# Layer 3 of a four-layer graph network: ScalarE's second measuring pass beside the propagation, and another order of copies and passes between the two steps

## Chip, cores and metric

The kernel runs on one core of one Trainium2 chip. The metric is device time in microseconds of one execution; the time before is the median of three executions. The profile is of one further execution.

## The reference, cut to what matters

Four layers follow one another, each as x = x + layer(relu(layernorm(x))), on N = 3327 nodes with D = 256 features. The change is in the fourth, called layer 3:

```python
def _top_p_attention(X, W1, W2, W3):
    logits = (X @ W1.T @ W2.T) @ (X @ W3.T).T
    probs = softmax(logits, axis=-1)
    # keep the largest probabilities of a row until their sum reaches 0.9
    A = probs * mask
    return A / max(A.sum(-1, keepdims=True), 1e-12)

R = (S + eye) / (S + eye).sum(-1, keepdims=True)     # S is adj
Z, Xf, Xa = 0, X, X
for n in range(2):
    A = _top_p_attention(Xa, W1, W2, W3)
    Xf = R @ Xf                       # propagation
    Xa = A @ Xa                       # attention
    Z = Z + Xf @ U1[n].T + Xa @ U2[n].T
out = layernorm(X + Z) * ln_g + ln_b
```

All arithmetic of these products is in float32.

## The kernel before

The nodes are padded to 3328 and cut into T = 26 blocks of 128 rows. A "row" below is such a block, m = 0 to 25. Layer 3 has two steps, 0 and 1, and every row of a step needs four pieces of work.

1. **Logits and exponentials.** `prepare` / `logits_steps`: TensorE multiplies queries and centred keys (L913) in four chunks, each into a two-bank PSUM tile `pl`; ScalarE takes the exponential of each chunk into the row tile `e` of 128 x 3328 with a running sum (L934). The tile pool `ps_row` behind `pl` has two buffers, which `pkq` (keys and queries of the next step), `u` (products with U1 and U2) and `pl` share.
2. **The search for the row's threshold.** `search_steps` is a generator with three stops. Up to the first stop, VectorE sums the row (`total`, L951) and ScalarE turns it into a first threshold `t` by four small activations with one VectorE operation between them (L952 to L956). Then comes ScalarE's first measuring pass, a Relu over the whole row (L967, `short`), and a second stop; then its second pass, a Sign over the whole row (L972, `sign`), and a third stop. In row 0 of a step, `alone` holds, and VectorE does the second one (L970). The rest is VectorE's: L977 to L980 improve the threshold, L983 measures again over the row, L992 and L996 mask the row in four parts and take the largest eight of each block, L1001 and L1004 take the largest forty, and L1012 applies the final threshold to `e`, the "mask" of the row.
3. **Attention.** `rows_times_steps` transposes `e` in 7 groups of up to four blocks on TensorE (L177) into PSUM, ScalarE copies each group to SBUF as `eT` (L180; three buffers, two PSUM buffers), and TensorE multiplies them with the values (L188). `Rows.begin` issues the first two groups' transposes, `Rows.finish` the rest.
4. **Propagation.** `propagated_steps` multiplies 26 blocks of the transposed adjacency with the features (L1068). SyncE's queue loads them in two slabs.

In step 0 the propagated row is scaled by ScalarE (`xf`, L1109), transposed and copied (`PropagationOfFirstStep.turn`, L138), and multiplied with U1 (`sums`, L1121; copied by ScalarE to `fsa`, L1123). The attention row is scaled (L1079), transposed and copied to `xT_a` (`AttentionOfFirstStep.turn`, L138), turned into keys and queries of step 1 (`node`; copies at L249 and L253 and a small DMA on ScalarE's queue), and multiplied with U2 (`values`).

**What sets the order.** Under `manual_schedule` TensorE's order is the order in which the code is traced. The orders of the other engines come from a planner that gives each instruction its place by estimated times and priorities; `high_priority` raises a priority. `issue_after(ins)` lets the instructions of its block stand only behind `ins` on its engine. `run(steps, at)` walks a generator and calls what `at` lists at a step number, so that other work is interleaved.

In step 0, rows 0 to 18 are "interleaved": `rows.finish(m)` runs together with the search of row m + 2, and then `propagate_first(m + 4)` together with the logits of row m + 3, at steps 0 and 12, the attention row's `turn` at step 3, `node` at 9, `values` at 18 and `rows.begin(m + 1)` at 20. Rows 19 to 25 have no propagation beside them except the last two. The function `passes` puts the search beside `rows.finish`: both passes each behind the newest `eT` copy, at steps 0 and 2, and VectorE's part at step 3.

Between the steps, the propagation of row 24 runs with the first logits of step 1, then a branch (`if_failed`) repairs rows whose search failed, and then the search of row 0 of step 1 and the propagation of row 25 follow, with the logits of rows 1 and 2 of step 1 at its steps 0, 6, 14 and 20. In step 1 each row does `rows.finish(m)` with a search, and then `propagate_second(m)` with the logits of row m + 3.

Of the kernel before, what the change touches and what calls it, by code (L numbers as in the profile page):

```python
# [16 lines left out]
AF = mybir.ActivationFunctionType  # L17
# [8 lines left out]
T = 26  # L26
NP = T * P
LAST = N - (T - 1) * P
NC = D // P
# [16 lines left out]
def kernel(  # L46
# [22 lines left out]
    nc = tc.nc  # L69
# [49 lines left out]
    def run(steps, at=None):  # L119

        for k in steps:
            for what in (at or {}).get(k, ()):
                what()

    def merged(*plans):
        out = {}
        for p in plans:
            for k, v in p.items():
                out.setdefault(k, []).extend(v)
        return out  # L130

    def transposed(src, pool, name):

        pt = ps_tr.tile([P, 4, P], F32, tag="tr", name=f"pt_{name}")
        for c in range(NC):
            nc.tensor.transpose(pt[:, c, :], src[:, c * P : (c + 1) * P], ident)
        dst = pool.tile([P, NC, P], F32, tag="xT", name=f"xT_{name}")
        nc.scalar.copy(dst, pt[:, :NC, :])  # L138
        return dst

    def search(es, t_bits, top_bit, measure, target, pool, name):
# [20 lines left out]
        nc.vector.scalar_tensor_tensor(eq, rank, n_tied, eq, ALU.is_lt, ALU.mult)  # L162
        nc.vector.scalar_tensor_tensor(e, eq, t, e, ALU.mult, ALU.add)

    last_turned = []
    GROUPS = [range(g, min(g + 4, T)) for g in range(0, T, 4)]

    def rows_times_steps(new_acc, e, rhs, pool, name):
# [671 lines left out]
    def layer_3_in(tag, big, ep, w3, sm3, h3, kT0, ksum0, left, at_end):  # L840
# [90 lines left out]

        def exp_of_logits(step, m, kT, e, parts, name=""):
            def evict(c, dst, src):
                nc.scalar.activation(dst, src, AF.Exp, accum_out=parts[:, c : c + 1])  # L934

            return logits_steps(kT, qT[:, m * P : (m + 1) * P], e, f"{name}{tag}{step}_{m}", evict)

# [332 lines left out]
        AHEAD = 3  # L1270
        EARLY = 4
        LATE = 3


        with tc.manual_schedule(engines=PE_ALONE):

            st0, made, dens, props = new_state("0"), {}, {}, []

            def prepare(step, m, kT):
                made[m] = scores(step, m, kT)  # L1280
                return made[m][2]

            def find(step, m, st):
                return search_steps(step, m, *made[m][:2], st, dens, m == 0)

            def passes(finder):


                if finder is None:
                    return {}  # L1290
                next(finder)

                def one_more():
                    with tc.issue_after(last_turned[-1].ins):
                        next(finder, None)

                return {0: [one_more], 2: [one_more], 3: [lambda: next(finder, None)]}

            def propagate_first(m, at):
                acc = new_acc(f"f0_{m}")  # L1300
                run(propagated_steps(acc, 0, m, h3), at)
                props.append(PropagationOfFirstStep(m, acc))

            def spread(steps, first=0, second=10):

                return {k: [lambda: next(steps, None)] for k in (first, second)}

            class Rows:


                def __init__(self, step, values):
                    self.step, self.values, self.begun = step, values, {}

                def begin(self, m):
                    if m < T:
                        name = f"a{self.step}_{m}"
                        accs = []

                        def acc():
                            accs.append(new_acc(name))  # L1320
                            return accs[0]

                        steps = rows_times_steps(acc, made.pop(m)[0], self.values, w3, name)
                        next(steps)
                        self.begun[m] = steps, accs

                def finish(self, m, at=None):
                    steps, accs = self.begun.pop(m)
                    run(steps, at)
                    return accs[0]  # L1330

            for i in range(EARLY):
                plan = {}
                if props:
                    p = props.pop(0)
                    plan = {5: [p.turn], 16: [p.sums]}
                if i == 0:
                    left.pool = w3, "eT", 3
                    propagate_first(0, dict(zip((14, 20), ([what] for what in left.stages))))
                    mean0 = key_sum(kT0, ksum0, "0")  # L1340
                elif i == 1:
                    steps = prepare(0, 0, kT0)
                    centred = {3: [lambda: centre(kT0, mean0(), "0")]}
                    propagate_first(1, merged(centred, spread(steps, 9, 19), plan))
                    run(find(0, 0, st0))
                else:
                    propagate_first(i, merged(spread(prepare(0, i - 1, kT0)), plan))
                    finder = find(0, i - 1, st0)
                    if i + 1 < EARLY:
                        run(finder)  # L1350
            p = props.pop(0)
            p.turn()
            p.sums()
            rows = Rows(0, h3)
            rows.begin(0)
            left_over = {}
            for m in range(T):
                plan = merged(passes(finder), left_over)
                if props:
                    p = props.pop(0)  # L1360
                    plan = merged(plan, {1: [p.turn], 5: [p.sums]})
                interleaved = m + EARLY < T - LATE
                steps = iter(())
                if m + AHEAD < T and not interleaved:
                    def begin_logits():
                        nonlocal steps
                        steps = prepare(0, m + AHEAD, kT0)
                        next(steps)

                    plan = merged(plan, {4: [begin_logits], 6: [lambda: next(steps)]})  # L1370
                a = AttentionOfFirstStep(m, rows.finish(m, plan), dens.pop(m), f"{m}")
                if interleaved:
                    left_over = {}
                    steps = prepare(0, m + AHEAD, kT0)
                    after = {3: [a.turn], 9: [a.node], 18: [a.values], 20: [lambda: rows.begin(m + 1)]}
                    propagate_first(m + EARLY, merged(spread(steps, 0, 12), after))
                elif m + 2 < T:
                    rows.begin(m + 1)
                    a.turn()
                    left_over = {0: [a.node], 2: [a.values]}  # L1380
                elif m + 1 < T:
                    left_over = {}
                    after = {1: [a.turn], 4: [a.node], 8: [a.values], 22: [lambda: rows.begin(m + 1)]}
                    propagate_first(T - LATE, after)
                finder = find(0, m + AHEAD, st0) if m + AHEAD < T else None


            flags0, mean1 = [], []

            def centre_second():  # L1390
                mean1.append(centre(kT1, total1(), "1"))

            def sum_second():
                nonlocal total1
                total1 = key_sum(kT1, ksum1, "1")

            def first_flags():
                with tc.high_priority():
                    flags0.extend(failed("0", st0))

            total1 = None
            steps = prepare(1, 0, kT1)
            propagate_first(T - LATE + 1, {
                1: [a.turn], 3: [first_flags], 4: [a.node], 8: [a.values, sum_second],
                11: [centre_second], 17: [lambda: next(steps)], 22: [lambda: next(steps)],
            })
            first_e, first_parts = made[0][:2]
# [17 lines left out]
        with tc.manual_schedule(engines=PE_ALONE):  # L1425
            st1 = new_state("1")
            run(find(1, 0, st1))
            p = props.pop(0)
            plan = {2: [p.turn], 10: [p.sums]}
            propagate_first(  # L1430
                T - 1, merged(spread(prepare(1, 1, kT1), 0, 6), spread(prepare(1, 2, kT1), 14, 20), plan)
            )
            run(find(1, 1, st1))
            finder = find(1, 2, st1)
            p = props.pop(0)
            p.turn()
# [8 lines left out]
            rows.begin(0)  # L1445
            flags1 = []
            for m in range(T):
                acc = rows.finish(m, passes(finder))
                y = attention_of_second_step(m, acc, dens.pop(m), f"{m}")
                plan = spread(prepare(1, m + AHEAD, kT1)) if m + AHEAD < T else {}  # L1450
                plan = merged(plan, {20: [lambda: rows.begin(m + 1)]})
                if m == T - 1:
                    plan = {4: [lambda: flags1.extend(failed("1", st1))]}
                finish3(m, y, propagate_second(m, plan), f"{m}")
                finder = find(1, m + AHEAD, st1) if m + AHEAD < T else None
# [79 lines left out]
```

## Time and profile before

| What | us |
|---|---|
| Median of 3 executions | 2659.49 (2658.65 to 2665.4) |
| The profiled execution, its own time | 2657.14 |
| Its span in the profile | 2655.3 |
| Period of a row in step 0 (rows 1 to 18) | 33.96 |
| Period of a row in step 1 (rows 4 to 22) | 29.31 |
| First transpose of row 0, step 0 | 1026.15 |
| First transpose of row 20, step 0 | 1689.40 |
| First transpose of row 0, step 1 | 1886.43 |

A period is the distance of the first transposes (L177) of two neighbouring rows. Times inside the execution count from the start of the span. In the timeline, a row has the start, the busy time, the engine, the line, the operation, what it writes and reads with shapes, how many instructions are merged, and in brackets the engine's idle time before it and what ended it. PE is TensorE's matmuls, PEld its weight loads, DVE VectorE, ACT ScalarE, POOL GpSimd, SP SyncE; a letter q marks an engine's instruction queue. A float32 matmul stands as two instructions.

### The profile page before, as it was taken

The numbers are of one execution on the slowest core, as the hardware profiler recorded it, in microseconds if no ns is written. First come the engines' busy times: TensorE is split into PE (matmuls) and PEld (weight loads), VectorE is DVE, ScalarE is ACT, GpSimd is POOL, SyncE is SP. The second block draws the span as 40 slices with busy tenths as digits, with TensorE's granted clock in tenths as the row PEclk, the third lists the DMA queues.
The fourth block names the chain that finished last, engine by engine and source line by source line (L and its number), as shares of the span: only waits on it lengthen the run. The fifth ranks groups of instructions, "written<-read, shape, count | busy, mean of one in ns | idle before, by whom it ended". The sixth has DMA issues, their size and how long they took to land. (4 is left out here: it accounts for less than half of the span.)

```text
span 2655.3 us, 42726 instructions
## 1 busy us (share of the span) xinstructions
PE 2575.5 (97%) x15979; PEld 2215.1 (83%) x15979; DVE 2050.0 (77%) x5495; ACT 1030.1 (39%) x1873; POOL 222.6 (8%) x435
## 2 busy tenths in 40 slices
PE   7999999999999999999999999989899999999997
PEld 6999999999999987777777777667677887888786
DVE  6667788888877849766666666893988888888882
ACT  2110134333011134555455555663554455445441
POOL 2000010000000000000000000000021112111111
PEclk9999999999999999999999999999999999999998
DMA  6555555555666631111111111001121122122211
GB/s 224 146 156 168 167 153 176 173 175 157 192 197 199 193 109 68 52 61 61 61 61 61 61 61 61 34 9 67 56 70 64 65 89 70 64 71 83 70 64 52
DMA packets 141359, 273.45 MB, mean 103 GB/s; under 512 B 15427, under 2 KB 67904, under 8 KB 141120
## 3 DMA queue, kind: packets, MB, share of 16 engines
q1 hardware_dynamic: 115648, 252.49, 29.8%
q10 hardware_dynamic: 25472, 17.92, 2.2%
q8 instruction: 132, 2.16, 0.3%
q14 instruction: 107, 0.88, 0.1%
HBM read 248.20 MB, written 20.45 MB: 101 GB/s over the span
## 5 line engine op out<-in xcount | busy, mean ns | idle before, releaser
L188 PE MATMUL a<-h3a,eT_a 128*128 128x256 f32 x1352 | 324.3, 381 | 12.4 <-ACT eT_a L180 11.0
L1068 PE MATMUL f<-h3a,slab3a 128*128 128x256 f32 x1352 | 326.9, 384 | 5.4 <-ACTq L1253 5.3
L188 PE MATMUL a<-vs,eT_a 128*128 128x256 f32 x1352 | 322.7, 383 | 1.1 <-ACT eT_a L180 0.9
L1068 PE MATMUL f<-fsa,slab3a 128*128 128x256 f32 x1352 | 312.7, 382 | 0.0
L1068 PEld LDWEIGHTS f<-h3a,slab3a 128*128 128x128 f32 x1352 | 247.3, 190 | 68.3 <-issue 30.9
L1068 PEld LDWEIGHTS f<-fsa,slab3a 128*128 128x128 f32 x1352 | 249.8, 189 | 52.7 <-issue 17.4
L188 PEld LDWEIGHTS a<-h3a,eT_a 128*128 128x128 f32 x1352 | 245.2, 189 | 53.9 <-ACT eT_a L180 21.5
L996 DVE MAX8 cand_a<-w 128x8 f32<-128x128 f32 x1352 | 281.9, 279 | 6.7
L188 PEld LDWEIGHTS a<-vs,eT_a 128*128 128x128 f32 x1352 | 246.1, 190 | 38.7 <-ACT eT_a L180 7.8
L519 PE MATMUL acc_a<-tsa,s_a 128*128 128x128 f32 (+1 forms) x2028 | 268.4, 275 | 0.7 <-DVE tsa L331 0.7
L180 ACT COPY eT_a<-pt_a 128x512 f32<-128x512 f32 (+1 forms) x364 | 195.0, 552 | 177.1 <-PE pt_a L177 173.6
L934 ACT ACTIVATE e_a<-pl_a 128x1024 f32<-128x1024 f32 x208 | 177.8, 860 | 198.3 <-PE pl_a L913 198.3
L519 PE MATMUL acc_a<-tsa,a_a 128*128 128x128 f32 x2028 | 250.3, 275 | 1.8 <-DVE tsa L334 1.8
L519 PE MATMUL acc_a<-rhs,a_a 128*128 128x128 f32 (+1 forms) x2028 | 250.4, 276 | 0.0
L519 PEld LDWEIGHTS acc_a<-tsa,s_a 128*128 128x128 f32 x2028 | 247.4, 192 | 1.2 <-DVE tsa L331 1.0
L519 PEld LDWEIGHTS acc_a<-tsa,a_a 128*128 128x128 f32 x2028 | 239.1, 192 | 3.1 <-DVE tsa L334 2.2
L519 PEld LDWEIGHTS acc_a<-rhs,a_a 128*128 128x128 f32 x2028 | 238.4, 192 | 1.9 <-ACT rhs L411 0.4
L992 DVE SCALAR_TENSOR_TENSOR w<-e_a,t_a 128x896 f32<-128x896 f32 x208 | 224.9, 1081 | 5.3
L177 PE MATMUL pt_a<-ident,e_a 128*128 128x128 f32 x1352 | 199.5, 273 | 1.8
L177 PEld LDWEIGHTS pt_a<-ident,e_a 128*128 128x128 f32 x1352 | 165.2, 140 | 39.5 <-ACT eT_a L180 9.5
L983 DVE SCALAR_TENSOR_TENSOR w<-e_a,t_a 128x3328 uint8<-128x3328 f32 x52 | 191.9, 3691 | 3.6
L1012 DVE SCALAR_TENSOR_TENSOR e_a<-e_a,all_least 128x3328 f32<-128x3328 f32 x52 | 192.1, 3695 | 1.2
(208 smaller groups left out, 3316.0 us busy)
## 6 DMA issues: line engine op xcount, KB each, us to landing
slab3a<-in_adj_t_dram SPq DMA_DIRECT2D x104, 832.0 KB, 5.9
a_a<-in_adj_t_dram SPq DMA_DIRECT2D x312, 256.0 KB, 3.4
a_a<-in_adj_t_dram SPq DMA_DIRECT2D x156, 320.0 KB, 3.5
x_dram<-x_a ACTq DMA_DIRECT2D x39, 256.0 KB, 2.8
x_a<-x_dram SPq DMA_DIRECT2D x26, 256.0 KB, 3.1
hT_dram<-xT_a ACTq DMA_DIRECT2D x26, 128.0 KB, 3.6
hT<-hT_dram SPq DMA_DIRECT2D x26, 128.0 KB, 2.1
z_dram<-z SPq DMA_DIRECT2D x26, 128.0 KB, 1.7
```

What stands on the lines that cost most here:

```text
L177: nc.tensor.transpose(pt[:, j, :], e[:, k * P : (k + 1) * P], ident)
L180: last_turned.append(nc.scalar.copy(eT[:, : len(blocks), :], pt[:, : len(blocks), :]))
L188: nc.tensor.matmul(acc[:, :width], ready[g][:, j, :], rhs[:, k, :], start=(k == 0), stop=(k == T - 1))
L519: nc.tensor.matmul(self.acc[:, g, at : at + wide], quads[n][:, k - CUTS[c][0], :], t, start=(k == 0 and n in (1, 4)), stop=(k == H - 1 and ...
L934: nc.scalar.activation(dst, src, AF.Exp, accum_out=parts[:, c : c + 1])
L983: nc.vector.scalar_tensor_tensor(junk, e, t, e, ALU.is_lt, ALU.mult, accum_out=got)
L992: nc.vector.scalar_tensor_tensor(w[:, : (b - a) * P], eg, t, eg, ALU.is_lt, ALU.mult, accum_out=below[:, g : g + 1])
L996: nc.vector.max(cand[:, 8 * k : 8 * k + 8], w[:, (k - a) * P : (k - a + 1) * P])
L1012: nc.vector.scalar_tensor_tensor(e, e, least, e, ALU.is_ge, ALU.mult, accum_out=st["kept"][:, m : m + 1])
L1068: nc.tensor.matmul(acc[:, :D], slab[g][:, j, :], xf[:, k, :], start=(n == 0), stop=(n == T - 1))
```

## The change

A function `passes_apart` takes the place of `passes` for the interleaved rows of step 0 and for rows 0 to 22 of step 1. The first pass stays beside `rows.finish`, at its step 0. The second pass, and the VectorE part behind it, go into the propagation that follows: in step 0 at its step 4, behind the newest copy that `transposed` made, in step 1 at its step 1, behind the newest exponential. Two lists hold those copies and exponentials.

Between the steps, `PropagationOfFirstStep(24)` (its scaling copy `xf` and its load of `hT`) is made after the branch and after the search of row 0, instead of before the branch. The search of row 1 is no longer traced after the propagation of row 25 but inside it: its sum and threshold at step 8 with high priority, its first pass there behind the newest exponential, its second pass at step 15 behind the newest exponential; only VectorE's part stays after the propagation. The `sums` of row 24 stay at step 10.

```diff
@@ -129,13 +129,15 @@
                 out.setdefault(k, []).extend(v)
         return out
 
+    last_copied, last_turned, last_exp = [], [], []
+
     def transposed(src, pool, name):
 
         pt = ps_tr.tile([P, 4, P], F32, tag="tr", name=f"pt_{name}")
         for c in range(NC):
             nc.tensor.transpose(pt[:, c, :], src[:, c * P : (c + 1) * P], ident)
         dst = pool.tile([P, NC, P], F32, tag="xT", name=f"xT_{name}")
-        nc.scalar.copy(dst, pt[:, :NC, :])
+        last_copied.append(nc.scalar.copy(dst, pt[:, :NC, :]))
         return dst
 
     def search(es, t_bits, top_bit, measure, target, pool, name):
@@ -162,7 +164,6 @@
         nc.vector.scalar_tensor_tensor(eq, rank, n_tied, eq, ALU.is_lt, ALU.mult)
         nc.vector.scalar_tensor_tensor(e, eq, t, e, ALU.mult, ALU.add)
 
-    last_turned = []
     GROUPS = [range(g, min(g + 4, T)) for g in range(0, T, 4)]
 
     def rows_times_steps(new_acc, e, rhs, pool, name):
@@ -931,7 +932,7 @@
 
         def exp_of_logits(step, m, kT, e, parts, name=""):
             def evict(c, dst, src):
-                nc.scalar.activation(dst, src, AF.Exp, accum_out=parts[:, c : c + 1])
+                last_exp.append(nc.scalar.activation(dst, src, AF.Exp, accum_out=parts[:, c : c + 1]))
 
             return logits_steps(kT, qT[:, m * P : (m + 1) * P], e, f"{name}{tag}{step}_{m}", evict)
 
@@ -1296,9 +1297,25 @@
 
                 return {0: [one_more], 2: [one_more], 3: [lambda: next(finder, None)]}
 
+            def passes_apart(step, finder):
+
+
+                if finder is None:
+                    return {}, {}
+                first = passes(finder)[0]
+
+                def second():
+                    with tc.issue_after((last_copied if step == 0 else last_exp)[-1].ins):
+                        next(finder, None)
+                    next(finder, None)
+
+                return {0: first}, {4 if step == 0 else 1: [second]}
+
             def propagate_first(m, at):
                 acc = new_acc(f"f0_{m}")
                 run(propagated_steps(acc, 0, m, h3), at)
+                if m == T - 2:
+                    return acc
                 props.append(PropagationOfFirstStep(m, acc))
 
             def spread(steps, first=0, second=10):
@@ -1355,11 +1372,12 @@
             rows.begin(0)
             left_over = {}
             for m in range(T):
-                plan = merged(passes(finder), left_over)
+                interleaved = m + EARLY < T - LATE
+                plan, later = passes_apart(0, finder) if interleaved else (passes(finder), {})
+                plan = merged(plan, left_over)
                 if props:
                     p = props.pop(0)
                     plan = merged(plan, {1: [p.turn], 5: [p.sums]})
-                interleaved = m + EARLY < T - LATE
                 steps = iter(())
                 if m + AHEAD < T and not interleaved:
                     def begin_logits():
@@ -1373,7 +1391,7 @@
                     left_over = {}
                     steps = prepare(0, m + AHEAD, kT0)
                     after = {3: [a.turn], 9: [a.node], 18: [a.values], 20: [lambda: rows.begin(m + 1)]}
-                    propagate_first(m + EARLY, merged(spread(steps, 0, 12), after))
+                    propagate_first(m + EARLY, merged(spread(steps, 0, 12), after, later))
                 elif m + 2 < T:
                     rows.begin(m + 1)
                     a.turn()
@@ -1400,7 +1418,7 @@
 
             total1 = None
             steps = prepare(1, 0, kT1)
-            propagate_first(T - LATE + 1, {
+            acc = propagate_first(T - 2, {
                 1: [a.turn], 3: [first_flags], 4: [a.node], 8: [a.values, sum_second],
                 11: [centre_second], 17: [lambda: next(steps)], 22: [lambda: next(steps)],
             })
@@ -1425,12 +1443,26 @@
         with tc.manual_schedule(engines=PE_ALONE):
             st1 = new_state("1")
             run(find(1, 0, st1))
-            p = props.pop(0)
-            plan = {2: [p.turn], 10: [p.sums]}
+            p = PropagationOfFirstStep(T - 2, acc)
+
+            def sum_of_second():
+                nonlocal second
+                second = find(1, 1, st1)
+                with tc.high_priority():
+                    next(second)
+                with tc.issue_after(last_exp[-1].ins):
+                    next(second)
+
+            def signs_of_second():
+                with tc.issue_after(last_exp[-1].ins):
+                    next(second)
+
+            second = None
+            plan = {2: [p.turn], 8: [sum_of_second], 10: [p.sums], 15: [signs_of_second]}
             propagate_first(
                 T - 1, merged(spread(prepare(1, 1, kT1), 0, 6), spread(prepare(1, 2, kT1), 14, 20), plan)
             )
-            run(find(1, 1, st1))
+            run(second)
             finder = find(1, 2, st1)
             p = props.pop(0)
             p.turn()
@@ -1445,10 +1477,11 @@
             rows.begin(0)
             flags1 = []
             for m in range(T):
-                acc = rows.finish(m, passes(finder))
+                plan, later = passes_apart(1, finder) if m + AHEAD < T else (passes(finder), {})
+                acc = rows.finish(m, plan)
                 y = attention_of_second_step(m, acc, dens.pop(m), f"{m}")
                 plan = spread(prepare(1, m + AHEAD, kT1)) if m + AHEAD < T else {}
-                plan = merged(plan, {20: [lambda: rows.begin(m + 1)]})
+                plan = merged(plan, {20: [lambda: rows.begin(m + 1)]}, later)
                 if m == T - 1:
                     plan = {4: [lambda: flags1.extend(failed("1", st1))]}
                 finish3(m, y, propagate_second(m, plan), f"{m}")
```

## The prediction

> **What bounds the kernel now.** I read the busy table first, then the mean row period from the first transpose of each attention row, and then the timeline of one row in each loop and of the stretches where TensorE stopped.
>
> ```profile
> PE 2575.5 (97%) x15979; PEld 2215.1 (83%) x15979; DVE 2050.0 (77%) x5495; ACT 1030.1 (39%) x1873; POOL 222.6 (8%) x435
> ```
>
> TensorE is the bound. So only the places where it pauses can give time, and ScalarE's 39% matters only where TensorE waits for a ScalarE copy. The timeline of a step-0 row (columns: start, busy, engine, line, operation, tiles, count, idle before and its cause) shows one such place:
>
> ```profile
> 1168.38 0.59 ACT L180 COPY eT_a<-pt_a 128x512 f32<-128x512 f32 x1 [0.53 <-PE pt_a L177]
> 1168.86 3.07 ACT L972 ACTIVATE junk_a<-e_a,t_a 128x3328 uint8<-128x3328 f32 x1
> ...
> 1170.29 1.89 PE L188 MATMUL a<-h3a,eT_a 128*128 128x256 f32 x8
> ...
> 1171.93 0.94 ACT L180 COPY eT_a<-pt_a 128x512 f32<-128x512 f32 x2
> ...
> 1172.06 0.15 DVE L977 TENSOR_SCALAR u_a<-sign_a 128x1 f32<-128x1 f32 x1 [9.23 <-ACT junk_a L972]
> ...
> 1172.56 1.99 PE L188 MATMUL a<-h3a,eT_a 128*128 128x256 f32 x8 [0.15 <-ACT eT_a L180]
> ```
>
> The second pass (L972) holds ScalarE for 3.07 us while the next block of transposes waits to be copied. Eight matmuls and four transposes take 2.16 us from start to start here, so eight and two should take 1.95; 1170.29 to 1172.56 is 2.27, and the restarted group loses another 0.10. The pass costs TensorE 0.42 us. In step 1 (from 2161.54 to 2163.66, 2.12 instead of 1.95, and 0.10 again) it costs 0.28. The first pass (L967) costs 0.31 and 0.15 and stays.
>
> Between the steps TensorE stops twice for long:
>
> ```profile
> 1844.86 0.47 ACT L1109 ACTIVATE xf<-f,rinv 128x256 f32<-128x256 f32 x1 [0.22 <-PE f L1068]
> 1850.13 1.22 PE L1068 MATMUL f<-h3a,slab3a 128*128 128x256 f32 x2 [5.30 <-ACTq L1253]
> ...
> 1868.66 0.20 ACT L952 ACTIVATE mean_a<-total_a 128x1 f32<-128x1 f32 x1 [7.34 <-DVE total_a L951]
> ...
> 1873.11 0.35 ACT L1123 COPY fsa<-u 128x256 f32<-128x256 f32 x1
> 1873.51 2.08 PE L913 MATMUL pl_a<-kT_1a,qT 64*128 64x512 f32 x4 [7.06 <-ACT fsa L1123]
> ```
>
> The first is the branch over the repair of failed rows. In the second the copy of u (PSUM, ready at 1863.7) stands behind row 1's search start and first pass, which wait for VectorE's sum; the logits need that bank.
>
> [...] the ready copy waited 9.4 us. [...] Here four logits matmuls after the 7.06 us wait took 2.08 us, where eight take 1.99. [...] the trace has 3.07, and I use that.
>
> **The change, part by part.** It adds no arithmetic, wait or transfer of its own; the pass stays one 3.07 us instruction and a 0.19 us accumulator read.
>
> *Step 0, rows 0 to 18.* The pass goes behind the copy of xT_a. There ScalarE is free from 1181.61 to the exponential at 1186.64, with 0.72 us of key and query copies and a 0.47 us DMA issue in between (key matmuls end near 1184.2). The pass would run 1181.6 to 1184.9: 4.4 of 5.0 us filled. Behind it the key copy comes 0.6 us late; who waits is the logits' fourth chunk, needing that bank near 1186.3, and the copies end by 1185.7. So the new place is free, with 0.6 us to spare. Row 0 lost 0.28, the others 0.42: 18 x 0.42 + 0.28 = **-7.8 us**. Bounds: -9 if first-pass waits shrink too, -3 if the key copies come late.
>
> *VectorE behind it.* Its search starts 12.7 us later. A row's mask is ready 29.6 us before its transposes, so 16.9 remain, and VectorE is busy 23.9 of 34 us. But rows 20 to 25 run closely:
>
> ```profile
> 1689.00:1800.00 111.00, 99.50 (x509) 75.25 (x506) 107.08 (x335) 67.70 (x126) 0.79 (x8) 1.00 0.03 8
> ```
>
> (columns: stretch, length, busy PE, PEld, VectorE, ScalarE, GpSimd, clock, DMA). VectorE is full here. Mask ends and transposes leave 17.6, 6.7, 5.5, 5.6, 1.0, 5.5 us for rows 20 to 25. On today's clock row 20's search, 24.4 us, would end at 1684.5 instead of 1671.8; row 21's could start at 1681.4 and now starts 3.1 later. Row 24 has 1.0 of room, so TensorE loses at least 2.1; if ScalarE's chain for the threshold (which waits for VectorE's sum with transposed blocks behind it) passes the delay on, 3.1. I take **+2.6**, bounds 0 (the planner finds a tighter order) and +5.
>
> *Between the steps.* Moving row 24's propagated copy past the branch lets ScalarE branch about 0.4 us earlier. Its 128 KB hT load moves too on SP's queue, and is needed at step 10 of the next propagation, some 11 us on: free. The copy now stands near row 0's threshold chain, up to 0.3 us. Row 1's start is pulled to step 8 with priority, and its second pass to after the next exponentials; the u copy can then go first. This removes the 7.64 us between matmul starts and about 1.6 of half clock, so with 0.4 TensorE could reach row 0's transposes (1886.43) 9.6 us earlier. But row 0's mask ends at 1879.84 on a VectorE that is continuously busy; with the same chain it ends near 1879.7, so TensorE starts at 1879.9: **-6.5 us**, and VectorE's mask is what is late next. Row 1's mask, now without row 2's scan in front, ends near 1879.7 + 24.5 = 1904.2; TensorE asks at 1907.6. Bounds: -9.6 and +1 (the copy still behind a pass).
>
> *Step 1, rows 0 to 22.* The pass goes behind the first two exponentials, between 2170.17 and 2174.49: 4.3 us for 3.3. The exponential behind it keeps its time. The mask comes 10.2 us later; of 20.4 us spare, 10.2 remain. 23 x 0.28 = **-6.4 us**; bounds -9 and -2. Rows 23 to 25 are unchanged; row 25's mask comes some 5 us late within 10.7.
>
> Sum: -7.8 + 2.6 - 6.5 - 6.4 = **-18.1 us**. The profiled execution took 2657.14 us (span 2655.3 and 1.84 around it) and would take 2639.0. The median of the runs shown is 2.35 above it, so I forecast 2659.5 - 18.1 = **2641.4 us**.
>
> **Rivals.** (1) *VectorE eats what ScalarE gives*: the tail costs its 5 us and the u copy stays behind the first pass, giving perhaps 2 us instead of 6.5. -7.8 + 5 - 2 - 6.4 = -11.2, 2648. The full VectorE in the tail speaks for it; the order written by hand between the steps speaks against. (2) *The planner moves waits rather than removing them*: only TensorE's order is written, and a rearranged ScalarE queue can cost a quarter microsecond per row elsewhere. 42 x 0.25 = 10.5 takes back most: 2652. For it: row 22's ScalarE idled 5.23 us ahead of a 0.20 us activation while TensorE waited. Against: in both loops VectorE waits for each pass and so falls into step anew. (3) *Slower: late thresholds hold the first transposed blocks.* With the search later, VectorE is in its scans when the next sum and threshold fall due:
>
> ```profile
> 2151.18 0.20 ACT L956 ACTIVATE t_a<-t_a 128x1 f32<-128x1 f32 x1 [0.39 <-DVE t_a L955]
> 2151.30 1.05 ACT L180 COPY eT_a<-pt_a 128x512 f32<-128x512 f32 x2
> ...
> 2152.74 1.89 PE L188 MATMUL a<-vs,eT_a 128*128 128x256 f32 x8
> ```
>
> The first copied block ends near 2151.9, its weight load starts at 2152.52: 0.6 us of margin. A threshold behind one scan and its maxima (1.15 + 0.08 + 1.45) is 2.7 late and costs 2.1 net; in 23 rows +48, or 2690. It decides above 8 us net loss once the excess passes (18 + 8)/23 = 1.1 us a row. Against: the sum falls due near 2176, behind a 3.69 us scan that ends near 2178.1, earlier than today's 2178.94. (4) *More*: if the threshold waits in the tail shrink as well (0.9 to 2.6 us each in four rows) and the tail costs nothing, -26: 2634. That the pass doesn't move would need ScalarE's order to ignore the edge written in the diff; I give it nothing.
>
> **Chances.** Forecast 0.64 (2636 to 2647), rival 1 0.14, rival 2 0.08, rival 3 0.08, rival 4 0.06. About 0.3%, 8 us, is what a measurement of this kernel can tell from no change. Faster by over that: 0.64 + 0.12 + 0.06 + 0.01 = 0.83; same 0.09; slower 0.08. The range 2632 to 2652 leaves out rival 3, part of rival 2 and the end of rival 4.
>
> **What would show it.** Step 0 row period 33.96 to 33.5; step 1, 29.31 to 29.03; the pass behind L138 and L934, and no TensorE wait at the last transposed block; row 20's mask about 5 us ahead of its transposes; the wait at L913 for the u copy under 2 us, with row 0's transposes right after its mask. The forecast is wrong if row periods don't shrink, if TensorE waits for transposed blocks at a row's start, or if the tail loses over 5 us.

## The result, and the profile after

The changed kernel takes **2648.44 us** (median of six runs, 2647.49 to 2649.88), the kernel before 2659.51 us (six runs, 2658.07 to 2665.4). The ratio is 0.9955, with a 95% interval of 0.9942 to 0.9967. The kernel is 11.1 us faster; the forecast was 18.1 us. The time lies inside the range of 2632 to 2652 us, but above the 2636 to 2647 that the prediction gave its own sum, and 0.4 us from the first rival's 2648.

The profiled execution after took 2649.88 us (span 2648.1), 1.4 us above its median, while the one before lay 2.4 us below its own. The two spans therefore differ by only 7.2 us. The rest is outside the change: row 0 of step 0 begins at 1026.15 us before and at 1030.48 us after, and ScalarE issues its instructions of layers 0 to 2 in the same order in both. In the eleven traces used here row 0 begins between 1026.15 and 1030.76 us. So all that follows is counted from the first transposes of row 0 of step 0, where layer 3's attention starts. I cut the trace there into stretches, each from the first transposes of one row to the first transposes of another (us; the last row is taken to the end of the last instruction):

| kernel | step 0, rows 0 to 19 | rows 19 to 25 | row 25 to row 0 of step 1 | step 1, rows 0 to 25 | to the end | sum | median of the runs |
|---|---|---|---|---|---|---|---|
| before | 641.26 | 142.29 | 76.74 | 724.64 | 44.19 | 1629.1 | 2659.5 |
| after | 633.49 | 146.87 | 75.84 | 717.21 | 44.20 | 1617.6 | 2648.4 |
| difference | -7.77 | +4.58 | -0.90 | -7.43 | 0 | -11.5 | -11.1 |
| predicted | -7.8 | +2.6 | -6.5 | -6.4 | 0 | -18.1 | -18.1 |

The two loops are as forecast. The stretch between the steps gave almost nothing, and the end of step 0 cost more.

Line numbers after are one higher than before from L177 to L1253 (L178, L181, L914, L935, L968, L973, L1013, L1124 answer to L177, L180, L913, L934, L967, L972, L1012, L1123), and L140 answers to L138's copy. The busy table:

```profile
PE 2567.5 (97%) x15979; PEld 2216.7 (84%) x15979; DVE 2032.5 (77%) x5495; ACT 1035.0 (39%) x1873; POOL 287.5 (11%) x435
```

All counts are those of before: nothing was added or removed, and ScalarE's busy time is 1035.0 us for 1030.1. In the timeline of a step-0 row (same columns as in the prediction), the pass now stands in the place that the diff names:

```profile
1183.62 0.37 ACT L140 COPY xT_a<-pt_a 128x256 f32<-128x256 f32 x1 [0.44 <-PE pt_a L138]
1183.89 3.07 ACT L973 ACTIVATE junk_a<-e_a,t_a 128x3328 uint8<-128x3328 f32 x1
...
1186.95 0.26 ACT L250 ACTIVATE kT_1a<-pkq 64x128 f32<-64x128 f32 x1
...
1189.02 1.02 ACT L935 ACTIVATE e_a<-pl_a 128x1024 f32<-128x1024 f32 x1 [1.45 <-PE pl_a L914]
```

It runs directly behind the copy of xT_a. The key copy behind it waits until 1186.95, and still ScalarE is idle for 1.45 us before the next exponential, because TensorE is what is late there. In step 1 the pass stands between the exponentials:

```profile
2165.44 1.01 ACT L935 ACTIVATE e_a<-pl_a 128x1024 f32<-128x1024 f32 x1
...
2166.44 3.07 ACT L973 ACTIVATE junk_a<-e_a,t_a 128x3328 uint8<-128x3328 f32 x1
...
2170.86 1.02 ACT L935 ACTIVATE e_a<-pl_a 128x1024 f32<-128x1024 f32 x1 [1.27 <-PE pl_a L914]
```

The group table says the same for all of step 1's attention matmuls at once (busy us, mean ns of one | idle before them, and what ended it). Before, this group had 1.1 us of idle time and a mean of 383 ns:

```profile
L189 PE MATMUL a<-vs,eT_a 128*128 128x256 f32 x1352 | 320.2, 381 | 0.2 <-ACT eT_a L181 0.2
```

Between the steps the timeline after shows why so little came:

```profile
1846.00 0.47 ACT L1110 ACTIVATE xf<-f,rinv 128x256 f32<-128x256 f32 x1 [0.23 <-PE f L1069]
...
1851.12 1.22 PE L1069 MATMUL f<-h3a,slab3a 128*128 128x256 f32 x2 [5.16 <-ACTq L1254]
...
1862.45 1.03 PE L1122 MATMUL u<-u1s,xT_f 128*128 128x256 f32 x4
...
1868.29 1.26 DVE L997 MAX8 cand_a<-w 128x8 f32<-128x128 f32 x6
1869.47 0.14 DVE L952 TENSOR_REDUCE total_a<-parts_a 128x1 f32<-128x5 f32 x1
...
1869.64 0.20 ACT L953 ACTIVATE mean_a<-total_a 128x1 f32<-128x1 f32 x1 [8.51 <-DVE total_a L952]
...
1871.03 3.07 ACT L968 ACTIVATE junk_a<-e_a,t_a 128x3328 uint8<-128x3328 f32 x1
...
1874.09 0.35 ACT L1124 COPY fsa<-u 128x256 f32<-128x256 f32 x1
...
1874.50 2.08 PE L914 MATMUL pl_a<-kT_1a,qT 64*128 64x512 f32 x4 [8.23 <-ACT fsa L1124]
```

The u product is complete near 1863.5. Its copy runs at 1874.09, because ScalarE's queue still has row 1's threshold chain and first pass in front of it, and the chain waits 8.51 us for a sum of 0.14 us that VectorE's queue holds behind row 0's third group of maxima. TensorE's logits then start at 1874.50 after a wait of 8.23 us (7.06 before). The scaling copy xf of row 24 also stands where it stood, ahead of the branch; TensorE's stop at the branch is 5.16 us, and was 5.30; over the eleven traces it is 4.69 to 5.33.

### The profile page after: what moved, and what is told of

The parts are those of the page before. It is cut to its first block, busy times and chain, and to the rows that moved or that the text cites. A ratio compares the mean times of both kernels' runs of the same rounds, so it can differ in the third digit from the quotient of the medians.

```text
span 2648.1 us, 42770 instructions
## 1 busy us (share of the span) xinstructions
PE 2567.5 (97%) x15979; PEld 2216.7 (84%) x15979; DVE 2032.5 (77%) x5495; ACT 1035.0 (39%) x1873; POOL 287.5 (11%) x435
## 5 line engine op out<-in xcount | busy, mean ns | idle before, releaser
L181 ACT COPY eT_a<-pt_a 128x512 f32<-128x512 f32 (+1 forms) x364 | 195.4, 553 | 330.4 <-PE pt_a L178 330.1
L935 ACT ACTIVATE e_a<-pl_a 128x1024 f32<-128x1024 f32 x208 | 177.7, 859 | 125.3 <-PE pl_a L914 125.3
L178 PE MATMUL pt_a<-ident,e_a 128*128 128x128 f32 x1352 | 199.5, 273 | 1.8
L178 PEld LDWEIGHTS pt_a<-ident,e_a 128*128 128x128 f32 x1352 | 165.4, 141 | 39.6 <-ACT eT_a L181 9.5
L1013 DVE SCALAR_TENSOR_TENSOR e_a<-e_a,all_least 128x3328 f32<-128x3328 f32 x52 | 191.6, 3685 | 1.9
```

What stands on the lines that cost most here:

```text
L178: nc.tensor.transpose(pt[:, j, :], e[:, k * P : (k + 1) * P], ident)
L181: last_turned.append(nc.scalar.copy(eT[:, : len(blocks), :], pt[:, : len(blocks), :]))
L935: last_exp.append(nc.scalar.activation(dst, src, AF.Exp, accum_out=parts[:, c : c + 1]))
L1013: nc.vector.scalar_tensor_tensor(e, e, least, e, ALU.is_ge, ALU.mult, accum_out=st["kept"][:, m : m + 1])
```

## Experiments: the parts alone

**Step 0 alone** (e1_s0). Between the steps and in step 1 the kernel is as before.

```diff
-                plan, later = passes_apart(1, finder) if m + AHEAD < T else (passes(finder), {})
+                plan, later = passes(finder), {}
...
```

> The kernel before with the change of step 0 alone: the second pass of rows 0 to 18 beside the propagation; step 1 and the stretch between the steps as before. In the traces the first transposes of rows 0 and 19 of step 0 lie 641.3 us apart before and 633.5 after the change, those of rows 19 and 25 142.3 and 146.9, row 25 to row 0 of step 1 76.7 and 75.8, rows 0 to 25 of step 1 724.6 and 717.2. If the parts are independent (my theory), this kernel shows 633.5 and 146.9 in step 0 and 76.7 and 724.6 behind it: 3.2 us less than before. If the later part of the change is what lengthens the tail (rival), rows 19 to 25 come back to 142.3 and it gains 7.8 us.

Measured: 2653.14 us, ratio 0.998 (0.9971 to 0.9989). Rows 0 to 19 take 633.49 us, -7.77 against before, and rows 19 to 25 take 145.64 us, +3.35. Everything else is within 0.5 us of before. So step 0's gain and its loss at the end both come from the step-0 edit alone. Summed as in the table, this kernel takes 3.74 us less than before, where 3.2 were expected; the interval of the ratio is a gain of 2.9 to 7.7 us.

**Step 1 alone** (e2_s1). Between the steps and in step 0 the kernel is as before.

```diff
-                plan, later = passes_apart(0, finder) if interleaved else (passes(finder), {})
+                plan, later = passes(finder), {}
...
```

> The kernel before with the change of step 1 alone: the second pass of rows 0 to 22 of step 1 behind the first two exponentials of the propagation. Theory: rows 0 to 25 of step 1 take 717 us instead of 724.6, since each row loses its 0.28 us wait for the last transposed block and two odd waits of the first rows go too; all else as before: 7.4 us less. Rival: the new order between the steps gave part of that, then step 1 takes 718 to 719 us and the gain is about 6.

Measured: 2651.32 us, ratio 0.9971 (0.9963 to 0.9979). Step 1 takes 717.22 us, -7.42; rows 19 to 25 take 142.28 us, as before. The two loops are independent of each other. In the sums of the stretches this kernel gains 7.54 us, so the two alone gain 11.28, and the whole change 11.50. What is left for the part between the steps is at most the 0.90 us of the table.

## Experiments: the end of step 0

**Row 20's search back in its old place** (e4_row18). `passes_apart` is left out for row 18 only, whose stretch carries row 20's search.

```diff
-                plan, later = passes_apart(0, finder) if interleaved else (passes(finder), {})
+                plan, later = passes_apart(0, finder) if m + EARLY + 1 < T - LATE else (passes(finder), {})
```

> The changed kernel, but in step 0's iteration 18 (the search of row 20) the second pass stays beside the attention rows as before. Theory: VectorE then begins the search of row 21 on time, and the tail, rows 19 to 25, takes about 142.5 us as before instead of 146.9, for 0.4 us more in iteration 18: 4 us less than the changed kernel. Rival: the tail is longer for another reason (another order of ScalarE's queue there, or a half-clock stretch after one wait), then it stays over 145 us.

Measured: 2644.03 us, ratio 0.9942 (0.9925 to 0.9958). Rows 19 to 25 take 142.87 us instead of 146.87, for 0.41 us lost in row 18. From the mask of row 20 to its transposes there are 14.9 us in this kernel, 4.8 us in the changed one and 17.6 before. So one late search, the first of the stretch in which VectorE is full (busy 107.08 of 111.00 us from 1689 to 1800 us before), makes 4.0 of the 4.6 us in these traces, and 2.8 of the 3.35 us with step 0 alone.

How the delay reaches TensorE is seen in the kernel with step 0 alone (timeline):

```profile
1723.15 3.69 DVE L1013 SCALAR_TENSOR_TENSOR e_a<-e_a,all_least 128x3328 f32<-128x3328 f32 x1
...
1726.76 0.42 DVE L1100 TENSOR_TENSOR z<-u,h3a 128x256 f32<-128x256 f32 x1
...
1727.24 1.13 PE L914 MATMUL pl_a<-kT_0a,qT 64*128 64x512 f32 x4 [0.95 <-DVE z L1100]
```

VectorE's addition z, which frees the PSUM bank of u, now stands behind a mask scan, and the logits wait 0.95 us for that bank. In the next row they wait 1.01 us. No wait of this kind is in the kernel before, nor in the one with row 20's search back. Their 1.96 us are the larger part of the 3.35. In the same stretch of this trace, eight matmuls behind a wait of 2.78 us take 2.70 us and the four transposes next to them 1.06 (2.00 and 0.60 at the same place of the changed kernel, behind a wait of 2.62 us and with a granted clock of 1.00), and TensorE's matmuls are busy 132.3 us for 130.7 before. Not all of that is a loss: in the changed kernel row 20 runs at full clock and still loses 2.03 us, against 2.40 here.

The changed kernel's +4.58 is 1.2 us more than the +3.35 of step 0 alone, and the stretch takes 145.53 and 145.52 us in two other kernels below that have the same step 0. The difference stands in row 23, which loses 1.38 us in the changed kernel and nothing in the others. It is a matter of the clock. In the changed kernel (timeline):

```profile
1769.19 0.20 ACT L957 ACTIVATE t_a<-t_a 128x1 f32<-128x1 f32 x1 [1.16 <-DVE t_a L956]
1769.48 3.07 ACT L968 ACTIVATE junk_a<-e_a,t_a 128x3328 uint8<-128x3328 f32 x1
...
1772.55 1.05 ACT L181 COPY eT_a<-pt_a 128x512 f32<-128x512 f32 x2
...
1773.17 3.57 PE L189 MATMUL a<-h3a,eT_a 128*128 128x256 f32 x8 [2.40 <-ACT eT_a L181]
```

Two transposed blocks wait behind a late threshold and its pass, TensorE waits 2.40 us, and the next eight matmuls take 3.57 us instead of 1.99; the granted clock is half from 1773.0 to 1776.4 us. With step 0 alone the same wait has the same length, and the eight matmuls take 1.99 us:

```profile
1770.02 1.99 PE L189 MATMUL a<-h3a,eT_a 128*128 128x256 f32 x8 [2.40 <-ACT eT_a L181]
```

## Experiments: between the steps

**The u copy first** (e3_ucopy). Row 1's start is traced behind the `sums`, and on ScalarE its threshold chain has an edge behind the u copy.

```diff
-                    nc.scalar.copy(fs[:, self.m, :], acc[:, :D])
+                    self.copied = nc.scalar.copy(fs[:, self.m, :], acc[:, :D])
...
-                with tc.high_priority():
+                with tc.high_priority(), tc.issue_after(p.copied.ins):
                     next(second)
...
-            plan = {2: [p.turn], 8: [sum_of_second], 10: [p.sums], 15: [signs_of_second]}
+            plan = {2: [p.turn], 10: [p.sums, sum_of_second], 15: [signs_of_second]}
```

> The changed kernel with one more edge: on ScalarE the threshold chain and first pass of row 1 of step 1 stand behind the copy of row 24's product u, which in the changed kernel stands behind them. Theory: the copy then runs when u is ready, near 1864 instead of 1874 us, and the 8.2 us wait of TensorE at the logits for it goes. The exponentials of row 2 still stand behind row 1's first pass, which waits for VectorE's sum near 1869.5 and ends near 1874, so TensorE gets a new wait of about 5 us at the third chunk of those logits: 3 to 4.5 us less than the changed kernel between the steps, row 0's transposes 1 to 2 us after its mask. Rival (VectorE is the bound there anyway): the mask of row 0 is late and nothing is gained. Rival (the wait is the bank's, not the queue's): the wait at the logits stays at 8 us.

Measured: 2645.91 us, ratio 0.9945 (0.9929 to 0.9962). Row 25 to row 0 takes 75.39 us, only 0.45 less than after, where 3 to 4.5 were expected. The timeline:

```profile
1860.22 0.37 ACT L1124 COPY fsa<-u 128x256 f32<-128x256 f32 x1 [2.38 <-PE u L1122]
...
1874.75 2.51 PE L914 MATMUL pl_a<-kT_1a,qT 64*128 64x512 f32 x8 [8.13 <-ACT e_a L935]
```

The copy now waits for nothing but TensorE. But row 2's exponentials stand behind row 1's first pass, and the pass behind the same late sum and threshold. TensorE waits 8.13 us for them instead of 8.23 us for the copy; about 5 were expected. The wait was moved.

**The exponentials in front too** (e5_order). Row 1's whole start is traced at step 15, behind the newest exponential.

```diff
-                with tc.high_priority():
-                    next(second)
                 with tc.issue_after(last_exp[-1].ins):
+                    with tc.high_priority():
+                        next(second)
                     next(second)
...
-            plan = {2: [p.turn], 8: [sum_of_second], 10: [p.sums], 15: [signs_of_second]}
+            plan = {2: [p.turn], 10: [p.sums], 15: [sum_of_second], 21: [signs_of_second]}
```

> The changed kernel, but on ScalarE the whole start of row 1's search in step 1 (threshold chain and first pass) stands behind the first two exponentials of row 2, so behind the copy of u and behind all that TensorE needs there; its second pass behind row 2's last exponentials. Theory: both 8 us waits (at the logits' bank for the copy, or for row 2's exponentials) and the half-clock stretch go, and TensorE is limited by row 0's mask on VectorE: row 0's first transposes come within 0.5 us of the mask's end, and row 25 of step 0 to row 0 of step 1 takes about 70 us instead of 75.8, 5 to 5.6 us less than the changed kernel. Rival: moving the chain back only makes another wait (row 25's scaling copy behind the late first pass), then 73 to 75 us and the transposes come 3 us or more after the mask.

Measured: 2651.31 us, ratio 0.9972 (0.9962 to 0.9982). Row 25 to row 0 takes 80.68 us, 4.8 more than after. The timeline:

```profile
1871.72 3.68 DVE L1013 SCALAR_TENSOR_TENSOR e_a<-e_a,all_least 128x3328 f32<-128x3328 f32 x1
...
1875.33 0.15 DVE L956 SCALAR_TENSOR_TENSOR t_a<-mean_a,c_a 128x1 f32<-128x1 f32 x1
...
1875.52 0.20 ACT L957 ACTIVATE t_a<-t_a 128x1 f32<-128x1 f32 x1 [10.48 <-DVE t_a L956]
...
1880.39 0.69 PE L138 MATMUL pt_f<-ident,xf 128*128 128x128 f32 x2 [12.36 <-ACT xf L1110]
```

Both earlier waits are gone. Now VectorE's threshold of row 1, one column and 0.15 us, stands behind row 0's rounds of maxima and mask scan. ScalarE waits 10.48 us for it with row 25's scaling copy queued behind, and TensorE waits 12.36 us for that copy. The rival, a wait that moves once more, was right, and the wait is longer than it gave.

**That order on a better loop** (e8_best). The edits of the last kernel with row 20's search back:

> The changed kernel with both e4_row18 and e5_order. Theory: the two are independent, 4 us from the tail and 5 from the stretch between the steps, 9 us less than the changed kernel: tail 142.9, between the steps 70, time near 2639 us. Rival: with row 0's mask as the bound between the steps, a shorter tail gives nothing more; then it is no better than e4_row18 by over 2 us.

Measured: 2650.99 us, ratio 0.9968 (0.9956 to 0.998). Row 25 to row 0 takes 80.74 us again and rows 19 to 25 take 142.90. The expected 70 us failed here too. The loss does not depend on when step 0 ends.

## Experiments: a better version

**The first pass beside the propagation too** (e6_first), in rows 0 to 17 of step 0, with row 20's search back. It goes behind the xT_a copy, and the second pass behind the newest exponential at step 13.

```diff
                 first = passes(finder)[0]
+                if step == 0:
+                    def behind(copies):
+                        def one():
+                            with tc.issue_after(copies[-1].ins):
+                                next(finder, None)
+                        return one
+                    return {}, {4: [behind(last_copied)], 13: [behind(last_exp), lambda: next(finder, None)]}
```

> The kernel of e4_row18 with the first pass, too, beside the propagation in rows 0 to 17 of step 0: the first behind the copy of xT_a, the second behind the last exponentials of the next row. Theory: the first pass's price beside the attention rows, 0.31 us a row, goes: the row period falls from 33.54 to about 33.2 us, rows 0 to 19 take 628 to 629 us instead of 633.9. The masks come 6.5 us later, within the 16 us there are, and the tail stays near 143 us. Rival: the second pass now stands ahead of the next row's threshold chain, which starts 1.6 us later and holds the first transposed blocks; then the period stays at 33.5 or grows.

Measured: 2638.84 us, ratio 0.9924 (0.9909 to 0.9939). The row period of step 0 is 33.22 us (33.54 after, 33.96 before), so the 0.31 us of the first pass, which the prediction read and left standing, is there to be had. Rows 19 to 25 take 142.28 us, as before. The timeline shows both passes in one propagation:

```profile
1178.99 3.07 ACT L968 ACTIVATE junk_a<-e_a,t_a 128x3328 uint8<-128x3328 f32 x1
...
1185.49 3.07 ACT L973 ACTIVATE junk_a<-e_a,t_a 128x3328 uint8<-128x3328 f32 x1
```

**The same with the exponentials in front between the steps** (e9_all):

> e8_best with the first pass beside the propagation as in e6_first. Theory: the gains add up, 14 us less than the changed kernel, near 2634 us. Rival as in e6_first: then no better than e8_best.

Measured: 2644.68 us, ratio 0.9942 (0.9928 to 0.9955). Rows 0 to 19 take 628.32 us as in the last kernel, row 25 to row 0 takes 80.87. The gains and the loss add up.

**Every queue between the steps in order of need** (e12_all). To the last kernel three edges are added. VectorE's last rounds and mask of row 0 stand behind row 1's threshold. Row 1's passes stand behind row 25's u copy. Row 2's threshold chain stands behind that copy as well. (`last_t` holds L956's instruction; `zeroth` is row 0's search, stopped ahead of its rounds. The diff is cut to the edges.)

```diff
             def sum_of_second():
                 nonlocal second
                 second = find(1, 1, st1)
                 with tc.issue_after(last_exp[-1].ins), tc.high_priority():
                     next(second)
+                with tc.issue_after(last_t[-1].ins):
+                    next(zeroth, None)
...
-            run(second)
-            finder = find(1, 2, st1)
             p = props.pop(0)
             p.turn()
             p.sums()
+            with tc.issue_after(p.copied.ins):
+                run(second)
+            finder = find(1, 2, st1)
...
+                with tc.issue_after(p.copied.ins) if not m else nullcontext():
                     plan, later = passes_apart(1, finder) if m + AHEAD < T else (passes(finder), {})
```

> The loops as in e6_first (first pass also beside the propagation in rows 0 to 17 of step 0, row 20's search where it was before) and another order between the steps, so built that no engine's queue has a long piece of work in front of a short one that TensorE waits for: row 1's sum, threshold and its ScalarE chain stand behind row 2's first exponentials; VectorE issues row 1's threshold (one column) before it goes into row 0's last five maxima and its mask scan; both of row 1's passes, and row 2's threshold chain, stand behind the copies of row 25 (xf and u) on ScalarE. The theory that TensorE waited only for such ScalarE copies, moved from one to the next, and that behind them stands VectorE's mask of row 0: no wait of 8 us or more is left, row 25's scaling copy comes within 1 us of its last propagation matmul, row 0's mask ends near 1875.5 on e5_order's clock and TensorE begins row 0's transposes within 1 us of it: row 25 to row 0 takes 70 to 71.5 us (e6_first 76.44, e5_order 80.68). Row 1's search now begins near 1876, so its mask is ready at about the time that TensorE asks for it (up to 2 us late). Layer 3 from row 0 on 1608.5 - 5 + 1 = 1603 to 1606, against 1608.5 for e6_first and 1629.1 before: about 2634 to 2637, ratio 0.991. Rival, that the wait moves once more: VectorE now stops for row 1's threshold or row 1's mask is several us late, so that the sum of the stretch from row 25 to row 1 is no better than e6_first's, and the time stays at 2639 or above.

Measured: **2637.43 us**, ratio 0.992 (0.9906 to 0.9934), the fastest median of all; its interval overlaps that of the version with both passes beside the propagation and the changed kernel's order between the steps, so that the two are not told apart by the medians. In the traces this one's stretches sum to 1605.9 us and the other's to 1608.5. Row 25 to row 0 takes 70.41 us, 6.33 less than before. The timeline (here L1015 is the mask scan and L178 row 0's transposes):

```profile
1865.80 3.69 DVE L1015 SCALAR_TENSOR_TENSOR e_a<-e_a,all_least 128x3328 f32<-128x3328 f32 x1
...
1869.55 1.97 PE L178 MATMUL pt_a<-ident,e_a 128*128 128x128 f32 x8 [4.06 <-DVE e_a L1015]
...
1871.34 3.78 PE L189 MATMUL a<-vs,eT_a 128*128 128x256 f32 x8
...
1874.91 1.04 PE L178 MATMUL pt_a<-ident,e_a 128*128 128x128 f32 x4
```

No wait of 8 us is left, and TensorE starts row 0's transposes within 0.1 us of the end of row 0's mask. The prediction's "VectorE's mask is what is late next" is thereby shown, for this order of the queues. But row 0 itself now takes 30.59 us instead of 27.38. TensorE has waited 4.06 us for the mask, and then runs at about half speed: eight transposes take 1.97 us (1.04 in the changed kernel), eight matmuls 3.78 (1.99), four transposes 1.04 (0.60). These come to 3.2 us, all of the 3.21 that the row lost. The expected delay of row 1's mask did not show: it ends at 1899.9, 0.2 us ahead of its transposes.

## Why the prediction was right in part

**Step 0's loop: right, mechanism and size.** -7.77 us for -7.8. The row differences between the two traces are 0.28 in row 0 and 0.42 in rows 1 to 18. The period fell from 33.96 to 33.54. A row's mask lies 16.4 us ahead of its transposes; 16.9 were worked out.

**Step 1: right, and a little small.** -7.43 us for -6.4; the period fell from 29.31 to 29.04. Twenty-one of the 23 rows gained 0.27 or 0.28 each. The others are row 1 with 0.46, which I have not followed, and row 2 with 1.21. In row 2 more than the pass was in the way before: ScalarE waited 4.95 us for the sum of a later row's threshold chain with the first transposed blocks behind it, and TensorE waited 0.67 us for them at 1947.46. After, that wait is gone. The prediction measured one steady row and took it for all; the first rows of a loop have to be read for themselves. The mask's lead is 8.8 us; 10.2 were worked out.

**The end of step 0: right in kind, mis-sized.** The term of +2.6 was +4.58, near its bound of +5. The reading (VectorE full, row 21's search 3.1 us late, one late search handed on from row to row) is what row 20's search put back shows; row 21's VectorE part begins 3.12 us later, counted from row 19's transposes. TensorE loses 3.27 us in rows 20 and 21, near the larger of the two values weighed, and 1.38 at half clock in row 23. It does not lose where the smaller value was worked out: row 24's mask lies 2.1 us ahead of its transposes, and was 1.0 ahead before. What the sum did not hold is the bank of u, freed by a VectorE addition that is queued behind the mask scan (waits of 0.95 and 1.01 us with step 0 alone), and the half clock after a wait (3.57 us for 1.99). Row 20's mask lies 4.8 us ahead; about 5 was given.

**Between the steps: wrong.** The step that failed is "the u copy can then go first". Of -6.5 only -0.90 came. The prediction took the diff to put row 1's first pass out of the u copy's way. In the diff, only the second pass goes behind the exponentials of row 2; the sum and the first pass are traced at step 8, ahead of the `sums` at step 10, and in ScalarE's order of the trace they stand ahead of the copy as before. The rival with the copy still behind the first pass had named this, at 2 us of gain; the prediction dismissed it with the words that the order here is written by hand. That order had to be read step by step.

Behind this lies a second mistake, which the traces of the kernels with the u copy first and with the exponentials in front show. Taking the copy out of the way would not have given the 6.5 us either. TensorE needed four things from ScalarE in this stretch (the u copy, two pairs of exponentials, row 25's scaling copy), and ScalarE was held by one-column results of VectorE. In this stretch of the changed kernel both engines took first what stood ahead in their queues: the u copy, ready near 1863.5 us, ran at 1874.09, though ScalarE was idle until 1869.64; and row 1's sum, whose last exponentials ended at 1861.1, ran on VectorE at 1869.47, behind row 0's maxima. Each repair of one queue uncovered the next wait: 8.23 us for the copy, 8.13 us for the exponentials, 12.36 us for the scaling copy. Only with all of them ordered did the stretch shrink, by 6.33 us. So the size of the gap was read rightly (the stretch takes 70.41 us, and 76.74 - 6.5 is 70.24), and the way to it was not what the change did. And not all of it is kept: 3.2 us go to TensorE's half speed after the wait of 4.06 us for the mask, a charge that the prediction made for the waits before and not for the new one.

**The branch: not there.** The 0.4 us supposed that the scaling copy of row 24 moves behind the branch. It runs at 1846.00 after, still ahead of it. The stop is 5.16 us for 5.30, and 4.69 with step 0 alone, where the order is the old one, so this difference is not the change's. Tracing an instruction later did not issue it later. A kernel that forces the copy behind the branch was not run, so what this move is worth stays open.

**The rivals.** The first, with its tail of +5 and -2 between the steps, comes to -11.2 against the measured -11.1, and both of its mechanisms were there. That the sum agrees so well is luck in part: its terms for the tail, the stretch between the steps and step 1 are off by 0.4, 1.1 and 1.0 us, in different directions. The others did not come: no quarter microsecond per row was lost elsewhere, and first transposed blocks do not wait in step 1 (0.2 us of idle time in the whole group).

## What to carry to other kernels

When a change reorders an engine's queue, list everything that a bottleneck engine takes from that queue in the stretch, and for each what stands ahead of it and what that waits for; a repair of one entry gives its time only when the next entries are free as well (here a wait of 8.23 us became one of 8.13, and then one of 12.36). A result of one column that another engine waits for belongs ahead of the long scans in its own queue (ScalarE waited 8.51 us for a sum of 0.14 us), and the gap in which a pass is to be hidden has to be checked for the rows where the cover ends, not only for the steady row. When the gain is a wait that becomes another wait, charge the slower matmuls after the new one too (3.2 us here).

## What the runs showed of the hardware that was not expected

TensorE slowed down after shorter waits than the 7.06 us for which the prediction had charged it, and not always. After the 4.06 us wait for row 0's mask with every queue in order of need, eight transposes took 1.97 us, for 1.04 in the changed kernel. After a wait of 2.40 us, eight matmuls took 3.57 us in the changed kernel, where the granted clock was half from 1773.0 to 1776.4 us, and 1.99 us with step 0 alone, with the same wait at the same place of the program. After a longer wait, 2.62 us, eight took 2.00 us at 1695.32 in the changed kernel and 1.99 us at 1745.06 in the kernel before, both at a granted clock of 1.00. So the length of the wait just before does not settle it in these traces.

In the trace of the changed kernel the clock was half in five stretches between 30 and 2610 us, of 3.41, 3.41, 3.41, 6.83 and 10.24 us. In the 3.41 us before each, TensorE's matmuls were busy for 1.14 to 1.55 us, by the profile's records (1.21 us before the one at 1773.0). In the kernel before it was half in two stretches of 6.83 us, each behind 3.41 us without a matmul. But from 1692.50 to 1695.91 in the changed kernel matmuls were busy for only 0.79 us, and the clock stayed full. What brings the half clock is not shown.
